# A stack of four graph layers on one core: a list scheduler at build time gives way to a fixed table of places, one round per graph

## The chip, the cores and the metric

The kernel runs on one NeuronCore of a Trainium2 chip. The metric is the device time in microseconds of one execution. Before the change it is 4071.69 us, the median of 3 runs (4068.57 to 4076.79). The five engines are TensorE (PE in the profile; PEld is its loading of weights), VectorE (DVE), ScalarE (ACT), GpSimd (POOL) and SyncE (SP), which here only issues transfers.

## The reference

32 graphs, each with 512 nodes of 256 features and a dense 512 x 512 matrix of edges, pass through four layers. Each layer adds to its input:

```python
h = maximum(layernorm(x), 0); x = x + gat_4_heads(h, adj, W0, a_src, a_dst)     # layer 0
h = maximum(layernorm(x), 0); x = x + gat_1_head(h, adj, W1, a)                 # layer 1
h = maximum(layernorm(x), 0); x = x + edge_scores(h, adj, a_0..a_3)             # layer 2
h = maximum(layernorm(x), 0); x = x + transformer(h, adj, Wqkv, Wo, W1, W2, ..) # layer 3

gat:         e = leaky_relu(s_i + d_j); softmax of e where adj > 0; attention @ (h W); elu
edge_scores: softmax of leaky_relu((h * a_k) @ h.T), k chosen by adj; attention @ h
transformer: 8 heads of 32 with mask, projection, layernorm, a feed-forward of 1024, layernorm
```

Everything is f32. No graph depends on another.

## The kernel before

All weights stay in SBUF. A graph is 481 *jobs*: a job is one instruction of VectorE, ScalarE or GpSimd, one transfer (or four of one kind) issued by SyncE, or a small group of matmuls. The Python function `quick_path` records the jobs of one graph after another through a `Plan`; nothing is issued while they are recorded. The functions `masks`, `layer0` to `layer3` inside `quick_path` record them, always in the same order, so the n-th job of each graph is the same piece of work.

The tiles that the text names:

- `ps_m` (4 jobs): bf16 transposes of the mask, each emptied by VectorE into `mT`; `m3` is the mask of layer 3.
- `ps_t`, `ps_t3`: f32 transposes of the normalized input (`h0`, `h1`, `h2`, `h3`, `n`); `ps_wh`: the products with W in layers 0 and 1.
- `ps_sp`, `rows`: a row of numbers is sent to DRAM and read back to all partitions (`rows0`, `rows1`).
- `ps_o`: attention times values in layers 0 (65 columns wide), 1 (`ps_o1`, 256) and 2 (`ps_o2`, 257); the profile leaves the number out. Before it stand VectorE's `p` (layers 0 and 1) and, in layer 2, the scores `ps_e` with ScalarE's `y`.
- `ps_qk`, `ps_v`, then eight times `ps_s`, `p` (two exponentials on ScalarE, one product with the mask on VectorE), `ps_to` (sums) and `ps_ct` (context): layer 3's attention. The sums go through DRAM twice to be inverted and spread: `to` -> `to_d` -> `part` -> reciprocal -> `in_d` -> `inv`, and VectorE multiplies `cT` by `inv`.
- `ps_wo`: the output projection, which needs `cT`; then `t`, its norm `n`, `ps_t3`, `tT`, the feed-forward `ps_f1` and `ps_f2` (both `ps_f` in the profile), `u`, `y`, and the transfer to the output.

Buffers come in *kinds* with a fixed number of slots, for instance three for `x` and `mT`, six for `p`, one for `h1`. The eight banks of PSUM are two slots `ps_a`, two slots `ps_b` of two banks each, and one each for `ps_ct` and `ps_to`. All matmuls of layers 0, 1 and 2, the mask transposes and `ps_f2` share the two `ps_a` slots; layer 3's share `ps_b`.

The order comes from `Plan.order`. It is a list scheduler that runs while the kernel is built. It keeps a clock for each engine and a queue of jobs whose predecessors are done, gives each job a duration (`takes`, `ends`), and lets a free engine take the ready job with the lowest key that finds its buffers free. The key is

```python
j.key = (self.start + self.done / self.work + self.later[self.at] / 1000, len(self.jobs))
```

that is, the number of the graph, the progress within a layer's stretch of matmul work, and a number from the table `LATER`, found in advance for each of the 481 jobs. Kinds marked `in_turn` give out their slots in the order in which they were recorded. `Plan.carry_out` then issues the jobs in the planned order of their start, ties each engine's instructions together in that order, and makes the first instruction of a new tenant of a slot wait for the first instruction of the one before. On the chip every engine runs its instructions in this fixed order and waits on semaphores for data of the others. At the end a check of ranges (`ok`) decides whether `general_path` must compute everything again; it does not run on these inputs.

Of the kernel before, what the change touches and what calls it, by code (L numbers as in the profile page):

```python
# [20 lines left out]
P = 128  # L21
# [79 lines left out]
class Home:  # L101


    def __init__(self, kind, name, shape, dtype):
        self.kind, self.name, self.shape, self.dtype = kind, name, shape, dtype
        self.tile, self.slot, self.uses, self.left, self.end, self.wants = None, None, [], 0, 0.0, []


class Kind:


    def __init__(self, pool, tag, slots, in_turn=True):
        self.pool, self.tag, self.in_turn = pool, tag, in_turn
        self.shared = tag in ("ps_a", "ps_b")
        self.free, self.last, self.queue, self.head = [0.0] * slots, [None] * slots, [], 0


class Job:
    __slots__ = ("key", "engine", "takes", "ends", "call", "left", "ready", "after", "homes", "start", "port", "moves")


class Plan:
# [4 lines left out]

    HOP = 0.15
    AGAIN = 0.04
    FIRST, LAST = 1.1, 0.25  # L130


# [5 lines left out]
    def __init__(self, tc, later):  # L138
        self.tc, self.nc, self.later = tc, tc.nc, later
        self.jobs = []  # L140
        self.graph()
        self.stage(0.0, 1.0)

    def graph(self):

        self.at = 0

    def stage(self, start, work):

        self.start, self.work, self.done = start, work, 0.0  # L150

    def tile(self, kind, name, shape, dtype=F32):
        home = Home(kind, name, shape, dtype)
        if kind.in_turn:
            kind.queue.append(home)
        size = int(np.prod(shape[1:]))
        return Part(home, np.arange(shape[0]), np.arange(size).reshape(shape[1:]))

    def put(self, engine, takes, ends, outs, ins, call, port=False, moves=None):


        j = Job()
        self.done += takes if engine == "PE" else 0.0
        j.key = (self.start + self.done / self.work + self.later[self.at] / 1000, len(self.jobs))
        self.at += 1
        j.engine, j.takes, j.ends, j.call, j.port, j.moves = engine, takes, ends, call, port, moves
        j.left, j.ready, j.after, j.homes, j.start = 0, 0.0, [], [], None
        before = set()
# [13 lines left out]

        for h in j.homes:
            if h.kind.shared:
                h.wants += [p.home for p in outs if p.home.kind.in_turn and p.home not in h.wants]
        for k in before:
            k.after.append(j)
        j.left = len(before)
        self.jobs.append(j)
        return j  # L190

    def behind(self, job, earlier):
        earlier.after.append(job)
        job.left += 1

    def order(self):

        engines = ("PE", "DVE", "ACT", "POOL", "SP")
        coming, waiting, free = ({e: [] for e in engines} for _ in range(3))
        free = dict.fromkeys(engines, 0.0)  # L200
        port, wire, now, begun = 0.0, 0.0, 0.0, []
        for j in self.jobs:
            if not j.left:
                heapq.heappush(coming[j.engine], (0.0, j.key, j))

        def slots(j):

            take, then = [], None
            need = [h for h in j.homes if h.slot is None]
            need = list(dict.fromkeys(need + [w for h in need for w in h.wants if w.slot is None]))  # L210
            for h in need:
                kind = h.kind
                if kind.in_turn and kind.queue[kind.head + sum(x.kind is kind for x, _ in take)] is not h:
                    return None, None
                open_ = [
                    s for s in range(len(kind.free))
                    if kind.free[s] <= now and not any(x.kind is kind and y == s for x, y in take)
                ]
                if not open_:
                    return None, [x for x in kind.free if now < x < 1e9]  # L220
                take.append((h, min(open_, key=lambda s: kind.free[s])))
            return take, None

        left = len(self.jobs)
        while left:
            moved, nexts = False, []
            for e in engines:
                if free[e] > now:
                    nexts.append(free[e])
                    continue  # L230
                while coming[e] and coming[e][0][0] <= now:
                    _, key, j = heapq.heappop(coming[e])
                    heapq.heappush(waiting[e], (key, j))
                put_back, j = [], None
                while waiting[e]:
                    key, one = heapq.heappop(waiting[e])
                    take, then = slots(one)
                    if take is not None:
                        j = one
                        break  # L240
                    put_back.append((key, one))
                    nexts += then or ()
                for one in put_back:
                    heapq.heappush(waiting[e], one)
                if j is None:
                    if coming[e]:
                        nexts.append(coming[e][0][0])
                    continue
                moved = True
                left -= 1  # L250
                for h, s in take:
                    h.slot = s
                    if h.kind.in_turn:
                        h.kind.head += 1
                    h.kind.free[s] = 1e9
                j.start = max(now, port) if j.port else now
                free[e] = j.start + j.takes
                if j.port:
                    port = free[e]
                begun.append(j)  # L260
                end = j.start + j.ends
                if j.moves is not None:

                    wire = max(wire, j.start + self.FIRST) + j.moves
                    end = wire + self.LAST
                again = free[e] if e == "PE" else end + self.AGAIN
                end += self.HOP
                for k in j.after:
                    k.left -= 1
                    k.ready = max(k.ready, again if k.engine == e else end)  # L270
                    if not k.left:
                        heapq.heappush(coming[k.engine], (k.ready, k.key, k))
                for h in j.homes:
                    h.left -= 1
                    h.end = max(h.end, end)
                    if not h.left:
                        h.kind.free[h.slot] = h.end
            if not moved:
                nexts = [x for x in nexts if x > now]
                assert nexts, "no job can begin"  # L280
                now = min(nexts)
        self.span = max(j.start + j.ends for j in begun)
        return sorted(begun, key=lambda j: j.start)

    def carry_out(self):
# [3 lines left out]
        for j in self.order():  # L289
            firsts = []  # L290
            for h in j.homes:
                if h.tile is not None:
                    continue
                kind = h.kind
                h.tile = kind.pool.tile(
                    h.shape, h.dtype, tag=f"{kind.tag}_{h.slot}", name=h.name, bufs=1
                )
                firsts.append((kind, h.slot))
# [33 lines left out]
    def dma(self, out, in_, moves):  # L332

        pairs = list(zip(out, in_)) if isinstance(out, list) else [(out, in_)]
        outs = [o for o, _ in pairs if isinstance(o, Part)]
        ins = [i for _, i in pairs if isinstance(i, Part)]
        real = lambda x: x.real() if isinstance(x, Part) else x
        call = lambda: [self.nc.sync.dma_start(real(o), real(i)) for o, i in pairs]
        return self.put("SP", 0.1 * len(pairs), 0.1, outs, ins, call, moves=moves)
# [27 lines left out]
def width(args):  # L367
# [5 lines left out]
LATER = [  # L373
    1743, 142, -2198, 582, -1342, -1423, -2322, 251, -1841, -1403, -2073, -1447, -1660, -546, -493, -862, 379,
    -874, -1735, -1387, -1078, -1245, 1879, 1934, 2313, 2511, 1421, 2599, 2919, 2849, 2122, 2830, 2624, 936,
    355, -400, 931, 2188, 1791, 389, 39, 1624, -2868, 2148, 1709, -920, 969, -2126, 2116, 2900, 2358, 686,
    -2280, 2546, 1408, 2128, 1465, -1811, 2793, 2937, 2731, 1331, -1834, -2962, -1606, 463, -492, 413, -2052,
    -1757, -198, 2759, 2862, 2931, 3000, 669, -1389, -2542, -2160, -1285, -764, 3000, 2630, 2553, 1961, 2215,
    -736, 91, 507, 1842, 626, 3000, 3000, 3000, 2743, 1127, -2304, -431, -1315, 528, 237, 2511, 2181, 2465,
# [989 lines left out]
```

## Time and profile before

| | before |
|---|---|
| time, median of 3 | 4071.69 us |
| span of the profiled run | 4075.2 us |
| mean granted clock of TensorE | 0.962 |
| TensorE busy | 3863.9 us, 95% |
| VectorE, ScalarE, GpSimd busy | 61%, 46%, 20% |
| transferred | 144.62 MB, 35 GB/s |
| matmul instructions | 20294 |

How to read it: an f32 matmul counts as two instructions. Busy time of TensorE contains no waits of more than the gaps shown, but it depends on the clock that was granted: the row PEclk of the page gives that clock in 40 slices of the span, in tenths of full speed. A group of instructions is named by line, engine and operation, with output and inputs. Lines 317, 338, 349 and 351 are the helpers through which all jobs of VectorE, ScalarE and GpSimd (317), all transfers (338), all transposes (349) and all products (351) are issued, so the tile's name tells the groups apart. In an order of time, the square bracket behind an instruction gives the idle time before it and what ended it.

### The profile page before, as it was taken

How to read it: one execution, taken by the hardware profiler on the slowest of the kernel's cores; microseconds unless marked ns; L12 is line 12 of the kernel's file. 1: busy time of each engine (PE TensorE's matmuls, PEld its weight loads, DVE VectorE, ACT ScalarE, POOL GpSimd, SP SyncE). 2: the span in 40 equal slices, each digit the busy share in tenths (PEclk: the TensorE clock that was granted, in tenths of full speed). 3: DMA queues.
4: the chain of work that ended last, by engine and by line, in shares of the span. 5: the costliest groups of instructions: out<-in, count | busy, mean ns of one | idle time of the engine just before them, and what ended most of it. 6: DMA issues, size and time to landing. Idle time of an engine off the chain costs nothing. (4 is left out here: it accounts for less than half of the span.)

```text
span 4075.2 us, 52142 instructions
## 1 busy us (share of the span) xinstructions
PE 3863.9 (95%) x20294; PEld 2427.2 (60%) x20294; DVE 2489.1 (61%) x5115; ACT 1881.6 (46%) x3297; POOL 828.8 (20%) x618
## 2 busy tenths in 40 slices
PE   5899999999999999999999999999999999999986
PEld 4655666655666655666655666655666655666543
DVE  4667656567666567656567656567656567656542
ACT  1345454445444445454445444445444445444442
POOL 0122122122122122122112122112122212122121
PEclk7899999999999999999999999999999999999998
DMA  3111101111101101101101101111101101100000
GB/s 111 42 32 43 32 29 40 37 32 43 32 30 40 37 32 43 32 29 40 37 32 43 32 30 40 38 32 43 32 29 40 38 32 43 32 24 24 17 11 13
DMA packets 99278, 144.62 MB, mean 35 GB/s; under 512 B 29008, under 2 KB 65360, under 8 KB 94928
## 3 DMA queue, kind: packets, MB, share of 16 engines
q1 hardware_dynamic: 92672, 136.22, 10.3%
q10 hardware_dynamic: 6352, 4.99, 0.4%
q8 instruction: 162, 2.65, 0.3%
q14 instruction: 92, 0.75, 0.1%
HBM read 122.96 MB, written 18.22 MB: 35 GB/s over the span
## 5 line engine op out<-in xcount | busy, mean ns | idle before, releaser
L351 PEld LDWEIGHTS ps_o<-wh,p 128*128 128x128 f32 x5120 | 696.9, 196 | 256.0 <-issue 189.0
L351 PE MATMUL ps_o<-wh,p 128*128 128x65 f32 (+1 forms) x5120 | 765.1, 302 | 15.7 <-DVE p L317 7.7
L317 DVE TENSOR_TENSOR p<-p,m 128x2048 f32<-128x2048 f32 x256 | 585.4, 2287 | 112.8 <-ACT p L317 112.6
L317 ACT ACTIVATE p<-ps_s 128x1024 f32<-128x1024 f32 x512 | 496.6, 1021 | 334.0 <-PE ps_s L351 333.9
L317 POOL TENSOR_SCALAR rstd<-mv 128x4 f32<-128x4 f32 x192 | 159.2, 829 | 1985.1 <-DVE mv L317 1950.7
L317 DVE SCALAR_TENSOR_TENSOR p<-rows,rt,mT 128x512 f32<-128x512 f32 x512 | 423.2, 868 | 116.3 <-DMA rows<-rows_d 58.1
L351 PE MATMUL ps_f<-ff_t,f 128*128 128x256 f32 x2048 | 489.0, 379 | 0.0
L351 PE MATMUL ps_f<-tT,ff_t 128*128 128x512 f32 x1024 | 465.4, 599 | 2.6 <-ACT tT L317 2.6
L351 PEld LDWEIGHTS ps_f<-ff_t,f 128*128 128x128 f32 x2048 | 377.2, 190 | 92.4 <-issue 39.0
L317 DVE TENSOR_TENSOR u<-ps_f,n 128x512 f32<-128x512 f32 x64 | 44.3, 692 | 524.9 <-PE ps_f L351 524.9
L351 PEld LDWEIGHTS ps_f<-tT,ff_t 128*128 128x128 f32 x1024 | 192.0, 193 | 206.9 <-issue 184.5
L317 ACT ACTIVATE h<-x,shift,rstd 128x256 f32<-128x256 f32 x512 | 265.6, 591 | 83.7 <-DVE x L317 36.5
L351 PE MATMUL ps_s<-qk 32*128 32x512 f32 x2048 | 296.2, 641 | 1.2 <-ACT p L317 1.1
L351 PE MATMUL ps_to<-p,ones 128*32 128x512 f32 x2048 | 272.1, 603 | 8.7 <-DVE p L317 8.7
L317 ACT ACTIVATE f<-ps_f,ff1b_c 128x512 f32<-128x512 f32 x256 | 161.7, 682 | 256.2 <-PE ps_f L351 256.2
L351 PE MATMUL ps_ct<-p,v 128*32 128x512 f32 x2048 | 269.7, 598 | 0.0
L351 PE MATMUL ps_e<-h2T,ha 128*128 128x512 f32 x512 | 262.4, 625 | 0.4 <-DVE o L317 0.4
L351 PE MATMUL ps_qk<-h3T,wqkv_t 128*128 128x512 f32 x512 | 242.9, 599 | 0.0
L351 PE MATMUL ps_o<-h,p 128*128 128x257 f32 x1024 | 238.3, 380 | 1.8 <-DVE x L317 0.9
L317 ACT ACTIVATE y<-ps_e,nshift 128x512 f32<-128x512 f32 x256 | 162.3, 688 | 126.1 <-PE ps_e L351 126.0
L351 PE MATMUL ps_wo<-wo_t,cT 128*128 128x256 f32 x512 | 192.9, 544 | 27.9 <-DVE cT L317 27.9
L317 ACT COPY wh<-ps_wh 128x258 f32<-128x258 f32 x128 | 47.7, 375 | 360.4 <-PE ps_wh L351 360.4
(114 smaller groups left out, 5021.8 us busy)
## 6 DMA issues: line engine op xcount, KB each, us to landing
adj<-in_adj_dram SPq DMA_DIRECT2D x32, 1024.0 KB
rows<-rows_d SPq DMA_DIRECT2D x32, 1024.0 KB
x<-in_x_dram SPq DMA_DIRECT2D x32, 512.0 KB
rows<-rows_d SPq DMA_DIRECT2D x32, 512.0 KB
inv<-in_d SPq DMA_DIRECT2D x256, 64.0 KB
out_dram<-y SPq DMA_DIRECT2D x32, 512.0 KB
ff_t<-in_L_gnn_W_dram ACTq DMA_DIRECT2D x2, 1024.0 KB
to_d<-to SPq DMA_DIRECT2D x64, 8.0 KB
```

What stands on the lines that cost most here:

```text
L317: return [getattr(unit, method)(*map(real, args), **{k: real(v) for k, v in kw.items()})]
L351: made.append(self.nc.tensor.matmul(*map(real, c[:3]), start=c[3], stop=c[4]))
```

## The change

The planner is gone. Each of the 481 jobs has a fixed *place*, the same for all graphs, in a table `PLACES` found in advance. A round is 100000 places long; graph number b is shifted by b rounds. The jobs are sorted by place and issued in that order. The places run from 0 to 503393, so that a graph is spread over five rounds and in a full round the jobs of five graphs interleave in one pattern that repeats. Slots are given in that order too: a new tenant takes, of the slots whose tenant has no use left, the one whose last use lies furthest back. The purpose is an order that is the same in each round and does not depend on a planner's durations.

```diff
-    def __init__(self, tc, later):
-        self.tc, self.nc, self.later = tc, tc.nc, later
+    def __init__(self, tc, table):
+        self.tc, self.nc, self.table = tc, tc.nc, table
         self.jobs = []
...
+    def graph(self, number):
+
+        self.number, self.at = number, 0
...
-        self.done += takes if engine == "PE" else 0.0
-        j.key = (self.start + self.done / self.work + self.later[self.at] / 1000, len(self.jobs))
+        j.place = (self.number * ROUND + self.table[self.at], self.at)
         self.at += 1
...
         for k in before:
+            assert k.place < j.place, "out of order"
             k.after.append(j)
...
-    def order(self):
...
-        for j in self.order():
+        for number, j in enumerate(sorted(self.jobs, key=lambda j: j.place)):
             firsts = []
             for h in j.homes:
-                if h.tile is not None:
-                    continue
-                kind = h.kind
-                h.tile = kind.pool.tile(
-                    h.shape, h.dtype, tag=f"{kind.tag}_{h.slot}", name=h.name, bufs=1
-                )
-                firsts.append((kind, h.slot))
+                if h.tile is None:
+
+                    kind = h.kind
+                    open_ = [s for s, x in enumerate(kind.homes) if x is None or not x.left]
+                    h.slot = min(open_, key=lambda s: kind.homes[s].used if kind.homes[s] else -1)
+                    kind.homes[h.slot] = h
+                    h.tile = kind.pool.tile(h.shape, h.dtype, tag=f"{kind.tag}_{h.slot}", name=h.name, bufs=1)
+                    firsts.append((kind, h.slot))
+                h.left -= 1
+                h.used = number
...
-LATER = [
-    1743, 142, -2198, 582, -1342, -1423, -2322, 251, -1841, -1403, -2073, -1447, -1660, -546, -493, -862, 379,
...
+ROUND = 100000
+PLACES = [
+    101057, 0, 123766, 132584, 138431, 138431, 129046, 129834, 141740, 143105, 134508, 134509, 144040, 210061,
...
     for b in range(B):
-        plan.graph()
-        plan.stage(b, 20.0)
+        plan.graph(b)
...
-        plan.stage(b + 1.3, 27.0)
         x_t = layer1(b, x_t, mT)
         layer2(b, x_t, mT)
-        plan.stage(b + 2.5, 70.0)
         layer3(b, x_t, m3)
```

Three of the durations that jobs carry were changed as well: the transfer of `rows` (1.25 + 0.5 n for 0.75 + 0.5 n), that of `inv` (0.9 for 0.75) and `ps_s` (1.25 for 1.15). Transfers gained the arguments `takes` and `how`, which no call sets.

## The prediction

> **What bounds the kernel now.** I read the page first, then the stretches of the span, then who waits for whom, and last the order of time in one round.
>
> ```profile
> PE 3863.9 (95%) x20294; PEld 2427.2 (60%) x20294; DVE 2489.1 (61%) x5115; ACT 1881.6 (46%) x3297; POOL 828.8 (20%) x618
> ...
> PEclk7899999999999999999999999999999999999998
> ```
>
> TensorE is the bound: 95% busy, the next engine 61%. Yet its granted clock is never a steady ten tenths. The table by stretch (length, then busy time of each engine, the granted clock after POOL) says where the rest lies:
>
> ```profile
> 0.00:200.00 200.00, 139.84 (x632) 111.06 (x633) 109.63 (x273) 54.34 (x122) 16.37 (x29) 0.80 0.24 78
> 200.00:3800.00 3600.00, 3503.88 (x18701) 2193.95 (x18701) 2280.96 (x4654) 1730.23 (x3023) 760.20 (x552) 0.98 0.11 35
> 3800.00:4075.20 275.20, 220.21 (x965) 122.16 (x963) 98.50 (x189) 97.03 (x153) 52.19 (x37) 0.90 0.05 14
> ```
>
> TensorE idles 60 us while the graphs fill the engines, 96 us in the 3600 us of repetition, 55 us while they drain. What it waits for between 300 and 3700 us (total, times, longest):
>
> ```profile
> PE ps_m L349 <- DVE mT L317: 25.9, 56, 0.7
> PE ps_m L349 <- DVE x L317: 21.5, 43, 0.7
> PE ps_wh L351 <- DVE wh L317: 15.8, 28, 0.6
> PE ps_wo L351 <- DVE cT L317: 15.1, 28, 1.1
> PE ps_wh L351 <- ACT h0T L317: 6.4, 28, 0.2
> PE ps_t L349 <- DVE mT L317: 5.7, 24, 0.2
> ```
>
> The sum is 90.4 us in 28 rounds, 3.2 us each, and all of it in one place of the round:
>
> ```profile
> 2086.08 0.40 PE L349 MATMUL ps_m<-ident_b,m 128*128 128x128 bf16 x4 [0.25 <-DVE x L317]
> 2087.13 0.40 PE L349 MATMUL ps_m<-ident_b,m 128*128 128x128 bf16 x4 [0.65 <-DVE x L317]
> 2087.78 0.38 PE L349 MATMUL ps_m<-ident_b,m 128*128 128x128 bf16 x4 [0.26 <-DVE mT L317]
> 2088.83 0.38 PE L349 MATMUL ps_m<-ident_b,m 128*128 128x128 bf16 x4 [0.67 <-DVE mT L317]
> ...
> 2090.97 5.78 PE L351 MATMUL ps_wo<-wo_t,cT 128*128 128x256 f32 x14 [0.43 <-DVE cT L317]
> ```
>
> The four mask transposes run with nothing between them, each waiting for VectorE to empty a bank; then the output projection waits for cT. And it is slow: 14 instructions in 5.78 us are 413 ns each, where 16 of ps_v, the same width, took 3.67 us, 229 ns each. The reason stands in the column after POOL:
>
> ```profile
> 2085.80:2089.20 3.40, 1.57 (x17) 0.97 (x16) 3.40 (x16) 1.79 (x2) 0.00 (x0) 1.00 0.21 64
> 2089.20:2092.60 3.40, 2.74 (x9) 2.08 (x9) 2.49 (x8) 0.00 (x0) 1.27 (x2) 0.50 0.89 274
> 2092.60:2096.00 3.40, 3.40 (x10) 2.68 (x9) 1.24 (x6) 0.00 (x0) 0.00 (x0) 0.50 0.15 55
> ```
>
> One stretch with TensorE 46% busy, and the next 6.8 us run at half clock. In them it is busy 2.74 + 3.40 = 6.1 us, so half of that, 3.1 us, is lost inside "busy" time. The waits cost twice.
>
> **What the Trainium skill says.** "TensorE: Matmul & The Clock Gate", Part 1, section "What's actually happening": the clock is full or half, half after an idle window of about 3.4 us, full again after a busy one. The trace agrees on two states and on the length (6.8 us are two windows), but the window that set it off was 46% busy, not idle. "DMA: Bandwidth & Descriptors", section on the anatomy of one DMA (for the path from gpsimd; here SyncE issues): about 2.0 us fixed, most of it the receipt. Here the copy "to" ended at 2081.52 and the reciprocal of "part", two transfers later, began at 2085.03: at most 1.75 us each. The same section says that the issuing sequencer does the waiting: a transfer that waits holds up those behind it in SyncE's queue.
>
> **The round, in terms.** The wait before ps_wo ends at 256.02 and at 2090.97 us, 15 rounds apart: 122.3 us a round. Less 3.2 idle and 3.1 half clock: 116.0 us of matmul at full clock. For 32 graphs 3712. The middle loses 29 x 6.3 = 183, so filling and draining lose 4075.2 - 3712 - 183 = 180.
>
> **The change, part by part.**
>
> *Removed: the planner at build time.* No instruction of a graph is added or dropped; the counts of matmuls, activations and transfers stay. The numbers handed to the transfers (1.25, 0.9) and to ps_s no longer decide anything, as the order ignores durations. Cost 0.
>
> *Moved: the mask transposes.* In the table the four ps_m stand at places 29046, 34508, 38431 and 41740 of a round, with ps_wo, ps_t, ps_wh and ps_t3 between them. The run of four gaps, 47.4 + 5.7 us over 28 rounds = 1.9 us a round, goes.
>
> *Moved: work into the wait for cT.* From the last ps_to of a graph to ps_wo runs one chain: copy, two transfers, reciprocal, two transfers, multiply. It took from 2080.68 to 2090.91, 10.2 us. Before, there is 5.1 us of matmul after that ps_to (to 2085.8), then the starved transposes. In the new order: two ps_ct (2 x 0.95), four jobs of ps_o2 (4 x 1.73), one ps_m (0.42), the half of ps_wo that needs the other cT (0.44): 9.7 us. So about 0.5 us of wait stays. The chain must not be held up: SyncE's queue has nothing between its four transfers that is late (the first cT's transfers come some 15 us of matmul earlier), and VectorE has x, e and statistics ahead of the reciprocal that end about when "part" lands.
>
> *New waits.* Nobody now takes a later job when one is late; each engine waits at the head of its queue. Behind the multiply that waits for the transfer stand mT, the reciprocals, x and h0T, which free the two ps_a banks. From there to the first ps_f1 VectorE has 53 instructions, 19.1 us by their means, beside 20.3 us of matmul. They follow each other faster than the means say, as they overlap:
>
> ```profile
> 29.77 1.40 DVE L317 BATCH_NORM_STATS2 st<-x 128x6 f32<-128x256 f32 x4
> ```
>
> That is 0.35 us each against a mean of 418 ns. At 0.07 us less each the 53 take 15.4 us. Following the banks in turn, I find gaps of 0.6 (ps_wo), 0.5 (a ps_wh behind t and statistics), 0.3 (ps_t3 behind ScalarE's n), 0.5 (ps_f1 behind tT), and some 0.4 in ps_e and attention: 2.3 us a round. With the full means as spacing it would be 4.6; with only the ps_wo wait, about 0.5. I take 2.3. No 3.4 us then has more than about 1 us idle, against 1.83 before, so I expect no half clock in the middle.
>
> *Fill and drain.* One graph enters per round. The five slices of a graph's matmul are about 0, 17, 15, 32 and 50 us, so full rounds begin after 116 us of matmul, where the old fill had done about 97 by its first ps_s (198 us, counted from the timeline): slice one ends about 68 us, when the timeline of before has the third head's p, as the first graph's chain is unchanged; slice two, with rows1 and p1, about 130; the third, 64 us of matmul with gaps, about 205. That is 89 lost, like before. In the drain attention runs alone in both orders (the old one needed 105 us for the last graph's). I leave 180.
>
> Sum: 3712 + 29 x 2.3 + 180 = 3959; the profiled run was 3.5 us above the median, so **3955 us**, 2.9% less.
>
> **The rivals.**
>
> *A, no loss in the middle is left* (0.3 a round): 3712 + 9 + 180 - 3.5 = 3897. For it: the waits named above vanish from the order. Against: the chain of 10.2 over 9.7, and VectorE's dense stretch.
>
> *B, the forecast, but strict rounds fill and drain worse*, by 60 us: 4015. For it: 89 us lost in fill rests on chains that I only added up; the old order could start a third graph early.
>
> *C, the gaps shrink but the half clock stays.* A stretch from 119.7 us, 88% busy (3.00 of 3.40) with nothing but small ps_o, was enough for it in the fill, and the new order has four ps_o jobs (3.6 us) in a row. 3712 + 29 x (2.3 + 3.1) + 180 - 3.5 = 4045.
>
> *D, slower.* Queues in fixed order jam in the dense stretch: 4.6 us of gaps, the half clock, and 30 us of worse fill: 3712 + 29 x 7.7 + 180 + 30 - 3.5 = 4142. For it: nothing reorders; VectorE is nearly full there. Against: the means overstate it.
>
> **How the numbers follow.** Forecast 0.53 (3925 to 3990), A 0.09, B 0.13, C 0.13, D 0.12. Faster is all but D and a little of C, which reaches to within 0.2% of 4071.7: 0.86, same 0.02, slower 0.12. The range 3900 to 4065 leaves out D and half of A.
>
> **What would show it.** Right: ps_m gone from the waits, the granted clock near 1.0 from 250 to 3750 us, ps_wo's mean down from 544 towards 390 ns, rounds of about 118.3 us, full rounds from about 205 us. Wrong: half clock once a round; a wait of over 2 us at ps_wo; or idle time of over 80 us before 250 or after the last full round.

## The result, and the profile after

| | before | after |
|---|---|---|
| time, median | 4072.15 us (4068.57 to 4076.79) | 3954.2 us (3954.0 to 3955.15) |
| after / before | | 0.971, interval 0.9693 to 0.9727 |
| span of the profiled run | 4075.2 us | 3952.2 us |
| one round, from a graph's first `ps_wo` to the next graph's, mean of 27 full rounds | 122.5 us | 117.8 us |
| rest of the span (span - 29 rounds) | 523 us | 535 us |

The round is 4.6 us shorter, 29 x 4.6 = 134 us; filling and draining cost some 11 us more. The page of after, first the row of busy times, then the granted clock in 40 slices:

```profile
PE 3784.1 (96%) x20294; PEld 2385.8 (60%) x20294; DVE 2592.2 (66%) x5115; ACT 1891.2 (48%) x3297; POOL 780.9 (20%) x618
...
PEclk7799999999999999999999999999999999999998
```

The slices of the clock look as before, since they are cut to whole tenths; the table by stretch (length, busy time of each engine, granted clock) tells the difference:

```profile
0.00:200.00 200.00, 127.53 (x561) 104.45 (x561) 104.13 (x256) 46.48 (x105) 13.54 (x26) 0.74 0.22 73
200.00:3800.00 3600.00, 3542.28 (x19276) 2221.61 (x19275) 2456.59 (x4803) 1799.17 (x3126) 737.91 (x573) 1.00 0.11 36
3800.00:3952.20 152.20, 114.34 (x458) 59.71 (x458) 31.46 (x60) 45.54 (x66) 29.43 (x19) 0.86 0.04 12
```

In the middle TensorE is idle for 58 us instead of 96, and its clock is full (1.00 for 0.98). The record of the clock in the two traces says the same: between 300 and 3700 us, before has 27 stretches at half clock, most of them 6.8 us long, and after has none. In the first 200 us it did 127.5 us of work where it did 139.8 before. What it still waits for between 300 and 3700 us (total, times, longest), 43.7 us in all, 1.6 a round where it was 3.2:

```profile
PE ps_wh L242 <- ACT rt L208: 14.0, 28, 0.5
PE ps_f L242 <- ACT tT L208: 10.7, 28, 0.4
PE ps_t L240 <- ACT h L208: 6.4, 28, 0.2
PE ps_wo L242 <- DVE cT L208: 5.8, 19, 0.5
PE ps_sp L240 <- ACT rt L208: 4.8, 28, 0.2
PE ps_wh L242 <- DVE h1T L208: 1.7, 1, 1.7
```

And the order of time where the starved transposes stood:

```profile
2033.80 5.49 PE L242 MATMUL ps_o<-h,p 128*128 128x257 f32 x24
2039.12 0.39 PE L240 MATMUL ps_m<-ident_b,m 128*128 128x128 bf16 x4
2039.34 0.65 PE L242 MATMUL ps_wo<-wo_t,cT 128*128 128x256 f32 x2
2040.16 0.70 PE L242 MATMUL ps_wo<-wo_t,cT 128*128 128x256 f32 x2 [0.17 <-DVE cT L208]
...
2048.22 1.16 PE L242 MATMUL ps_wh<-w_t,h0T 128*128 128x264 f32 x4 [0.50 <-ACT rt L208]
```

So 1.6 of the 4.6 us a round come from shorter waits; the other 3.0 are about what the half clock cost, which the prediction put at 3.1. In the round shown, the wait for cT is 0.17 us where it was 0.43 behind 1.83 us of other waits. The group of `ps_wo` takes 396 ns an instruction instead of 544, that of `ps_m` idles 9.9 us in all instead of 60.8.

### The profile page after: what moved, and what is told of

Same layout as the page of the kernel before. It is cut to its first block, busy times and chain, and to the rows that moved or that the text cites. A ratio compares the mean times of both kernels' runs of the same rounds, so it can differ in the third digit from the quotient of the medians.

```text
span 3952.2 us, 51981 instructions
## 1 busy us (share of the span) xinstructions
PE 3784.1 (96%) x20294; PEld 2385.8 (60%) x20294; DVE 2592.2 (66%) x5115; ACT 1891.2 (48%) x3297; POOL 780.9 (20%) x618
## 5 line engine op out<-in xcount | busy, mean ns | idle before, releaser
L242 PEld LDWEIGHTS ps_o<-wh,p 128*128 128x128 f32 x5120 | 707.4, 198 | 251.2 <-issue 184.9
L242 PE MATMUL ps_o<-wh,p 128*128 128x65 f32 (+1 forms) x5120 | 762.5, 303 | 27.1 <-DVE p L208 27.1
L208 POOL TENSOR_SCALAR rstd<-mv 128x4 f32<-128x4 f32 x192 | 105.4, 549 | 2490.0 <-DVE mv L208 2197.7
L242 PE MATMUL ps_f<-tT,ff_t 128*128 128x512 f32 x1024 | 455.5, 600 | 13.7 <-ACT tT L208 13.7
L242 PE MATMUL ps_f<-ff_t,f 128*128 128x256 f32 x2048 | 457.6, 380 | 0.0
L208 ACT ACTIVATE h<-x,shift,rstd 128x256 f32<-128x256 f32 x512 | 275.1, 593 | 206.8 <-DVE shift L208 121.7
L242 PE MATMUL ps_e<-h2T,ha 128*128 128x512 f32 x512 | 254.0, 619 | 2.5 <-ACT y L208 1.9
L242 PEld LDWEIGHTS ps_o<-h,p 128*128 128x128 f32 x1024 | 188.9, 189 | 79.5 <-issue 54.5
L208 POOL TENSOR_TENSOR rstd<-rstd,nhalf 128x4 f32<-128x4 f32 x192 | 208.3, 1089 | 13.4
L208 DVE BATCH_NORM_STATS2 st<-x 128x6 f32<-128x256 f32 x512 | 205.6, 414 | 8.1 <-DMA x<-in_x_dram 4.9
```

The source lines that it names most:

```text
L208: return [getattr(unit, method)(*map(real, args), **{k: real(v) for k, v in kw.items()})]
L242: made.append(self.nc.tensor.matmul(*map(real, c[:3]), start=c[3], stop=c[4]))
```

## The experiments

The interval is that of the ratio to the kernel before, which ran again beside each group of experiments; its medians lie between 4071 and 4075 us. Round and rest are those of the profiled run, as above; the rest is good to some 2 us.

| | time (us) | ratio | round | rest |
|---|---|---|---|---|
| e1 old pattern, fixed places | 4113.35 | 1.0081 to 1.0119 | 122.5 | 561 |
| e2 e1, transposes spread | 4178.87 | 1.0239 to 1.0279 | 124.5 | 569 |
| e3 e1, two `ps_o2` ahead of them | 4110.16 | 1.007 to 1.011 | 122.4 | 564 |
| e4 both | 4151.45 | 1.0176 to 1.0213 | 123.4 | 571 |
| e5 before, transposes three times | 4030.38 | 0.987 to 0.9922 | 121.0 | 519 |
| e6 after, transposes three times | 3983.18 | 0.9752 to 0.9803 | 118.9 | 534 |
| e7 e4, layer 1's front moved too | 4233.4 | 1.0376 to 1.0416 | 126.3 | 571 |
| e8 planner with the places as keys | 3955.1 | 0.970 to 0.9738 | 118.2 | 525 |
| e9 after, transposes in a run | 4024.33 | 0.9865 to 0.9903 | 120.1 | 538 |
| e10 after, one multiply later | 4034.23 | 0.9883 to 0.9923 | 120.2 | 549 |
| e11 after, layer 1's front later | 4261.42 | 1.0451 to 1.0488 | 128.0 | 545 |
| e12 e8, strict in the middle | 3939.44 | 0.966 to 0.9693 | 117.1 | 543 |

**e1: is it the fixed places, or the pattern?** The planner's order repeats itself in the middle. Folded into one round it gives a table for the new code, with the old pattern.

```diff
-ROUND = 100000
-PLACES = [101057, 0, 123766, ...
+ROUND = 1000000
+PLACES = [the planned starts of one graph, as parts of a round]
```

> The fixed table, but with the places that the planner's own repeating round has (all 481 jobs in the old order, one graph per round). Theory (two spots of the round decide: the run of mask transposes, and too little matmul beside the chain to cT; the half clock follows from both): as the kernel before, about 4080 us (4050 to 4110), ps_m run with gaps, half clock once a round. Rival 1 (a fixed order with slots taken by last use is what helps, not the pattern): 3950 to 3985. Rival 2 (the run of mask transposes alone is the cause): as the theory here.

The round is that of the kernel before to 0.1 us, with the same waits and the same half clock; the 38 us that e1 takes more (the kernel before took 4074.99 beside it) are all in the rest (561 for 523). So fixed places by themselves gain nothing in the middle and cost 1%, 3 us above the theory's range: the first `ps_wo` comes at 270.6 us instead of 246.7. What the change gains comes from the pattern in its table; e8 shows the other half of this.

**e2, e3, e4: is the run of transposes the cause?** Two traits of the new table were put into e1's (the last six digits are the place within the round).

```diff
 # e2: of the four ps_m and their copies, one stays, three go between jobs of ps_wo; the making of m3 goes behind them
 # e3: two jobs of ps_o2 and their readers on VectorE go ahead of the run
 # e4: both
-    ps_m    10: 1330421,  8: 1336332,  4: 1345390      (most of ps_wo: 355143 to 377030)
+    ps_m    10: 1359500,  8: 1370500,  4: 1378000
-    ps_o2  243: 3419067, 246: 3448385      ps_m  6: 1321456
+    ps_o2  243: 3318000, 246: 3326400      ps_m  6: 1328450
```

> As the run before, but three of the four mask transposes moved between the jobs of ps_wo, so that they no longer form a run (their copies and m3 follow them). Theory: nothing gained, since the transposes had stood in the wait for cT: the gap before ps_wo grows from 0.4 to about 4 us a round and the half clock stays: 4060 to 4120 us. Rival 1: as the old pattern within 15 us. Rival 2: gaps and half clock go, 3950 to 3985 us.

> As the old pattern, but the two jobs of ps_o2 that stood behind ps_wo moved ahead of the run of mask transposes (3.5 us of matmul under the chain to cT); the run stays. Theory: the wait for cT goes, the four gaps of the run (1.8 us) stay, and with them the half clock in most rounds: 4010 to 4070 us. Rival 1: as the old pattern within 15 us. Rival 2: as the old pattern within 15 us.

> Both moves at once in the old pattern. Theory: no run of gaps, no wait over 1 us before ps_wo, no half clock in the middle: 3950 to 3990 us, all of the gain from some 20 of 481 places. Rival 1: as the old pattern within 15 us. Rival 2: as the spread alone.

e2, what TensorE waited for:

```profile
PE ps_wo L242 <- DVE cT L208: 85.3, 27, 3.4
PE ps_wh L242 <- DVE wh L208: 23.9, 27, 0.9
```

Spread alone makes it 65 us slower than e1, past the theory's range: the transposes had covered some of the chain to cT, and 3.2 us a round are now spent in one piece. In e3 the wait for cT is gone, and the half clock is down to 15 stretches of 3.4 us. Yet the time is e1's, for new waits take back what that gains; the two jobs had been covering another chain:

```profile
PE ps_t L240 <- ACT n L208: 32.4, 27, 1.2
PE ps_m L240 <- DVE x L208: 20.2, 27, 0.8
PE ps_f L242 <- ACT tT L208: 18.5, 27, 0.8
```

These are 1.2 us a round for the normalized `n` and 0.7 for `tT`, where e1 shows neither. e4 has hardly any half clock left (1.00 in the middle) and still takes 123.4 us a round: 5.9 us of waits, most of them on cT, n, wh, x, tT and f. Its expectation, a time near the new table's, failed altogether. The run of transposes was a place at which the old order's lack of matmul showed; taking it out alone made things worse.

**e5, e6: what is the half clock worth?** Each mask transpose is issued three times, with the same result. That only adds work.

```diff
-plan.matmuls(0.7, *((ps[:, i], m[:, i, cut(j, P)], ident_b) for i in range(NT)))
+plan.matmuls(0.7, *((ps[:, i], m[:, i, cut(j, P)], ident_b) for _ in range(3) for i in range(NT)))
```

> The kernel before, its order untouched, each mask transpose issued three times (the same result written again): 8 more small matmuls in each of four jobs a round, some 0.5 us each by the spacing of transposes. Theory (the clock halves because a 3.4 us window is less than half busy): more work makes the round shorter; the repeats fall largely into the gaps, the half clock goes: 3990 to 4040 us. Rival (the clock halves for another reason, or bf16 transposes do not count as activity): 1 to 2.2 us a round more, 4100 to 4140 us.

> The kernel after with the same repeats, the price of the repeats where no gap takes them: about 2 us a round by theory and rival, 4005 to 4030 us.

In the new order, where TensorE has hardly a gap there, the added work costs 29 us, 1.1 a round (118.9 for 117.8), less than expected. In the old one it takes 42 us off. The middle of e5:

```profile
200.00:3800.00 3600.00, 3517.51 (x19767) 2221.33 (x19768) 2293.87 (x4709) 1747.91 (x3064) 770.89 (x562) 1.00 0.11 35
```

Its clock is 1.00 where it was 0.98: much of the work lies in the gaps, and of the 27 stretches at half clock four are left, of 3.4 us each. "TensorE: Matmul & The Clock Gate" of the Trainium skill (Part 1, "What's actually happening") speaks of idle windows; here a stretch that was half busy was enough, and filling it with useless work paid. e6 alone would have called the transposes a cost.

**e7: is cover for the second chain what e4 lacks?**

```diff
 # on e4: layer 1's front into the stretch between ps_wo and ps_f1
-    h1 123: 2470173   ps_t 127: 2671763, 132: 2522135   ps_wh 140: 2741122, 146: 2711956, 143: 2686421, 137: 2733826
+    h1 123: 2380000   ps_t 127: 2410800, 132: 2407200   ps_wh 140: 2416000, 146: 2418500, 143: 2425500, 137: 2428000
```

> The kernel of e4 (the old pattern as a fixed table, mask transposes spread, two of the ps_o2 jobs moved) with one more of the new table's traits: layer 1's front, the transposes of h1 and the products with h1T (8 small groups of matmul, about 5.4 us), moves into the stretch between ps_wo and the first ps_f1 of another graph. Theory: what was missing in e4 is matmul to lie over two chains at once, the one from the sums to cT and the one from t over its norm to tT. Then the waits of a round fall from 5.8 to about 2.5 us, no half clock comes back, and the time is about 4055 us (4010 to 4080), 70 to 140 below e4; it stays above the new table's, for the strict rounds of the old pattern lose some 40 us in the fill (e1 against the kernel before). Rival: the queues of VectorE and ScalarE jam in that stretch whatever matmul lies beside it: 4140 or more.

The theory fails by 150 us; the time lies on the rival's side (4140 or more). The wait for `n` is gone from the list, as the theory had it, but cT still takes 34.2 us in 27 rounds and wh 25.0, and h0T (22.4) and h1T (17.6) are new. For cT the trace gives the reason: the transfer of `inv` was issued at 2048.83 us, in the new table's kernel 3.45 us pass from that to the multiply, but here the multiply began at 2054.20, 5.4 us later. It stood in VectorE's queue behind readers of `ps_o2`, a mask copy and statistics. That led to e10.

**e10: one instruction's place in VectorE's queue.** TensorE's order is the new table's; only VectorE's queue is changed (the last five digits are the place within the round).

```diff
 # new table, VectorE around the multiply of cT (job 363, place 429525)
-     7: 129834, 250: 329903, 251: 331583, 256: 331714, 254: 332413, 257: 333807
+     7: 129300, 250: 329310, 251: 329320, 256: 329330, 254: 329340, 257: 329350
```

> The new table with one place changed in effect: on VectorE the multiply of cT with inv, which the second half of ps_wo waits for, stands behind the readers of the last ps_o2 bank, the copy of the first mask and three statistics instead of ahead of them, as it stands in the kernel of e7. TensorE's order stays as it is. Theory (the place of the waiting multiply in VectorE's queue decides the wait at ps_wo, and e3, e4 and e7 lost by it): ps_wo waits 1.3 to 2 us a round where it waits 0.2, most of it not made good later: 3980 to 4005. Rival (TensorE's order alone matters, and VectorE catches up): under 3965.

The order of time on VectorE, in after:

```profile
2039.41 0.69 DVE L208 TENSOR_TENSOR cT<-cT,inv 128x512 f32<-128x512 f32 x1 [0.74 <-DMA inv<-in_d]
2040.02 0.42 DVE L208 COPY mT<-ps_m 128x512 bf16<-128x512 bf16 x1
2040.36 0.16 DVE L208 RECIPROCAL inv<-ps_o 128x1 f32<-128x1 f32 x1
```

and in e10, where the last transfer was issued at 2078.22, so that inv is there at about 2078.22 + 3.45 = 2081.67:

```profile
2081.80 0.42 DVE L208 COPY mT<-ps_m 128x512 bf16<-128x512 bf16 x1 [0.86 <-PE ps_m L240]
2082.14 0.16 DVE L208 RECIPROCAL inv<-ps_o 128x1 f32<-128x1 f32 x1
2082.34 0.48 DVE L208 SCALAR_TENSOR_TENSOR x<-ps_o,inv,x 128x256 f32<-128x256 f32 x1
2082.74 1.07 DVE L208 BATCH_NORM_STATS2 st<-x 128x6 f32<-128x256 f32 x3
2083.72 0.68 DVE L208 TENSOR_TENSOR cT<-cT,inv 128x512 f32<-128x512 f32 x1
```

```profile
2084.45 0.70 PE L242 MATMUL ps_wo<-wo_t,cT 128*128 128x256 f32 x2 [2.21 <-DVE cT L208]
```

The multiply is 2.05 us late, and `ps_wo` waits 2.2 us for it where it waited 0.2. Most rounds take 119.8 us, 2.0 more than in after: all of the lateness reaches the end, and nothing is made good later. Every fifth round has 3.4 us of half clock behind the wait besides and takes 121.5, so that the mean is 2.3 more. The whole is +80 us, twice what was expected; 67 of it is 29 x 2.3, the rest is in the fill and the drain.

**e9: the transposes put back in a run, in the new table.**

```diff
-     6: 129046, 10: 134508, 4: 138431, 8: 141740
+     6: 129046, 10: 129070, 4: 129090, 8: 129100      (each with its copy behind it)
-     250: 329903, 251: 331583      (VectorE's readers of the last ps_o2 bank)
+     250: 329060, 251: 329061
```

The copies and the two readers then stand ahead of the multiply of cT in VectorE's queue, so this run holds a part of e10's change too.

> The new table with one thing undone: the four mask transposes stand in a run ahead of ps_wo again, each with VectorE's copy of its bank behind it and the copies ahead of the multiply that makes cT, as in the kernel before. All other places stay. Theory (the run starves TensorE on VectorE's copies and sets off the half clock): some 1.7 us more idle a round at ps_m and ps_wo, a stretch of 3.4 us about half busy, and half clock after it, 3 us more: 3954 + 29 x (1.7 to 4.7) = 4003 to 4090, about 4070. Rival (what the new table gains lies in the rest of its order, and the run costs little in it): under 3985.

```profile
2079.33 0.38 PE L240 MATMUL ps_m<-ident_b,m 128*128 128x128 bf16 x4 [0.52 <-DVE mT L208]
2079.92 0.71 PE L240 MATMUL ps_m<-ident_b,m 128*128 128x128 bf16 x8 [0.21 <-DVE x L208]
2080.47 0.65 PE L242 MATMUL ps_wo<-wo_t,cT 128*128 128x256 f32 x2
2081.82 0.70 PE L242 MATMUL ps_wo<-wo_t,cT 128*128 128x256 f32 x2 [0.69 <-DVE cT L208]
```

The gaps come back, 0.52 and 0.21 at `ps_m` and 0.69 at `ps_wo`, and the time is 70 us longer, on the theory's side. The half clock comes only in every fourth or fifth round, which then takes 121.5 us instead of 119.8. What TensorE waited for at these places, between 300 and 3700 us:

```profile
PE ps_wo L242 <- DVE cT L208: 19.6, 28, 0.9
PE ps_m L240 <- DVE mT L208: 14.4, 28, 0.5
PE ps_sp L240 <- ACT rt L208: 12.8, 28, 0.5
```

With 5.9 us of `ps_m` behind x, 20 us are gaps in the run itself. The 14 us more at `ps_wo` need not be the run's: in the round shown `inv` was issued at 2075.27, so that it was there at about 2078.72, and the multiply began at 2081.10, behind the copies, 2.4 us late as in e10. So in the old pattern spreading the run costs 65 us, and in the new one a run costs something, at most 70; how much of that is the run and how much the late multiply, this run doesn't separate.

**e11: layer 1's front out of the stretch, in the new table.**

```diff
-    123 to 148: 233629 to 240610 (between ps_wo and ps_f1), the row after them 245207
+    123 to 148: 244500 to 249735 (between the ps_f1), the row after them 250200
```

> The new table with layer 1's front (the four activations h1, the transposes of h1, the products with h1T, the row after them) moved from between ps_wo and the first ps_f1 to between the ps_f1, so that 5.4 us of matmul no longer lie beside the chain t, n, ps_t3, tT. Theory (the new order is fast because the chains are covered by other graphs' matmul): ps_t3 and ps_f1 wait some 4 us more a round, and the half clock may come back: 3954 + 29 x (3.5 to 7) = 4055 to 4157, about 4100. Rival (the chain gets shorter by as much, as VectorE and ScalarE lose the work of h1 there): under 4000.

```profile
PE ps_t L240 <- ACT n L208: 50.4, 26, 1.9
PE ps_wh L242 <- DVE h1T L208: 22.7, 26, 0.9
PE ps_wh L242 <- ACT rt L208: 20.4, 26, 0.8
PE ps_f L242 <- ACT f L208: 18.5, 11, 1.7
PE ps_o L242 <- DVE p L208: 18.0, 27, 0.7
```

The wait for `n`, absent in after, is 1.9 us in each round, and the clock falls to 0.97 in the 3600 us of the middle, by which some 100 of the 307 us are half clock (an estimate: 0.03 x 3600). But the theory's 4 us at `ps_t3` and `ps_f1` are 2.2, and the time is 160 us above its middle: most of the waits are where the front now stands (h1T, p, f). The run shows that the front can't be moved by a tenth of a round; it doesn't separate the missing cover from the crowd at the new place.

**e8, e12: a faster version.** e8 is the old list scheduler with the new places as keys; slots are given out in the order of the places too.

```diff
-j.key = (self.start + self.done / self.work + self.later[self.at] / 1000, len(self.jobs))
+j.key = (self.number * ROUND + PLACES[self.at], self.at)
```

> The old list scheduler with the new table's places as its keys: a free engine may take a later job when the one in turn isn't ready, so the first and last rounds are filled greedily, while the repeating part keeps the new table's order but for some 6 inversions a round on TensorE, 31 on ScalarE and 150 on VectorE. Theory: strict rounds cost the fill some 20 to 40 us, and the order by place is what makes the middle fast: 3920 to 3950. Rival: the planner's durations are off in the middle, so the exchanges on VectorE bring waits back, 1 to 3 us a round: 3960 to 4020, with the fill shorter all the same.

Its rest is that of the old kernel (525), and it loses 0.3 us a round, so that nothing is left: 3955.1, between the theory and its rival. Together with e1 this settles where the gain lies: the old scheduler reaches the new time with the new places, and the new code keeps the old round with the old ones. e12 keeps each engine strictly in order of place from place 360000 to 3350000, and moves layer 3's weights, with the few instructions that prepare them, from ScalarE's queue to SyncE's.

```diff
+if FROM <= j.key[0] < TO:
+    if j.engine in last: self.behind(j, last[j.engine])
+    last[j.engine] = j
...
-    nc.scalar.dma_start(t, ap)       # wqkv, wo, ff1, ff2 and layer 3's vectors
+    nc.sync.dma_start(t, ap)         # issued behind the first graph's input
```

> An attempt at a faster version. The places as in the new table, strict on every engine from the fourth round to the last graph's, but the first and last rounds filled by the old list scheduler with the places as keys (as in e8, where the repeating part lost 0.3 us a round by being reordered as well); and the weights of layer 3 are fetched by SyncE behind the first graph's input instead of by ScalarE, whose first activation of a graph waited until 25.1 us for the issue of all of them. Expected: 7 us from the first graphs, 3 from the last, 5 from the weights: 3936 to 3948. Rival (a gain in the fill is swallowed by the next graph's wait, as in e8): 3950 to 3957.

The time came in as expected, 3939.4, the fastest of all, and for another reason: the rest is 543 us, 8 more than after, and the round is 117.1 us, 0.8 less. The weights gained nothing. The first graph's `ps_sp` runs at 30.5 instead of 36.5 us, but the row it sends goes through SyncE's queue with small weight transfers on both sides:

```profile
32.26 0.35 SPq L366 DMA_DIRECT2D rows_d<-spr  x1
32.65 0.42 SPq L40 DMA_DIRECT2D b_c<-in_L_gnn_ln_b_dram  x1
...
34.10 0.43 SPq L40 DMA_DIRECT2D g_r<-in_L_gnn_ln_g_dram  x1
34.63 0.38 SPq L366 DMA_DIRECT2D rows<-rows_d  x1
```

VectorE's first `p`, which needs it, began at 42.06 us, against 43.21 in after: 1.1 of 6 us are left. From the issue of `rows` to `p` it took 7.4 us (34.63 to 42.06), in after 4.7 (38.47 to 43.21), and from the issue of `rows_d` to that of `rows` 2.4 us instead of 1.4. Whether the queue or the DMA engines themselves held the row up, the run doesn't show: from 32 to 43 us the engines were 71% busy.

The shorter round comes from one stretch. From the second half of `ps_wo` to the first `ps_f1` TensorE takes 16.3 us in after (2040.16 to 2056.42) and 15.5 in e12 (2149.32 to 2164.80), which is the whole 0.8. What differs there is when ScalarE waits. In after:

```profile
2047.31 0.18 ACT L208 ACTIVATE wh<-ps_wh 128x4 f32<-128x4 f32 x1 [0.31 <-PE ps_wh L242]
2047.98 0.18 ACT L208 ACTIVATE rt<-ps_wh 128x8 f32<-128x8 f32 x1 [0.49 <-DVE wh L208]
```

and in e12:

```profile
2156.03 0.18 ACT L345 ACTIVATE wh<-ps_wh 128x4 f32<-128x4 f32 x1 [0.31 <-PE ps_wh L379]
2156.10 0.18 ACT L345 ACTIVATE rt<-ps_wh 128x8 f32<-128x8 f32 x1
```

Both engines read one bank of `ps_wh`, and they take turns in the order in which the program issues them. The table has VectorE's product `wh` (place 135221) ahead of ScalarE's `rt` (135696), so ScalarE, which waits in order, stands still for 0.49 us four times a round, and `ps_wh`, `ps_t` and `ps_sp` wait behind it (0.50, 0.23 and 0.17 us in after). e12 issues by planned start, `rt` first; each engine's own order is unchanged, and these waits of TensorE are gone but for 0.36 us behind VectorE. "PSUM — Partial Sum Buffer" ("PSUM bank collisions raise a hardware error") says that the compiler puts a dependency between two engines' accesses to one bank, reads by ScalarE and VectorE alike; the 0.49 us fit that. The exchange of the two places alone was not run, so that it makes the whole 0.8 us is not shown; e12 also gives out its slots differently.

## Why the prediction was right

3955 was forecast and 3954.2 measured. That it is right to 1 us is luck, for three small errors cancel. The gaps were smaller than forecast, 29 x (1.8 - 2.3) = -15 us for the profiled span (1.8 is the round of 117.8 less 116.0 of matmul). Fill and drain were larger, 3952.2 - 3712 - 29 x 1.8 = 188 for 180. And the 3.5 us taken off at the end were a trait of the one profiled run of before, the slowest; in after the span is 2.0 us below the median, 5.5 us the other way. What holds is the mechanism: the run of gaps and the half clock go, and small waits take their place.

- *116.0 us of matmul a round*: holds; 117.8 less the 1.6 us of waits is 116.2.
- *The run of transposes goes, and the half clock with it*: holds in after, where `ps_m` is out of the list and the middle runs at 1.00. As a cause by itself it is too simple. e2 shows that taking out the run alone makes the old pattern slower; e9 shows that with the rest of the new table in place it is worth something: 20 us of gaps are its own, and 70 us is the most.
- *A chain of 10.2 us over 9.7 us of matmul, 0.6 of wait at ps_wo*: it waited in 19 of 28 rounds, 0.2 us on average. The condition that the prediction put beside it, that the multiply must not be held up, carried the result: e10 breaks it and loses 80 us, and e9 breaks it too.
- *The other gaps*: `ps_f1` behind tT 0.4 for 0.5. `ps_wh` 0.5 for 0.5, but not because VectorE's queue is dense with statistics: it is the turn-taking at the bank, which the prediction didn't know. `ps_t3` behind `n` none for 0.3, attention none for 0.4; `ps_t` behind h (0.2) and `ps_sp` behind rt (0.2) were not foreseen. That the sum came close owes something to luck.
- *Nobody takes a later job when one is late*: right, and seen in e10, where 2 us of lateness cost 2.0 us in most rounds and half clock besides in every fifth.
- *The fill*: full rounds were forecast from about 205 us, at a loss of 89; by the places they began at about 235, at a loss of 119 with the same 116 us of matmul (the slices that the prediction names add up to 113). In the fill TensorE waits 27.1 us for `p` behind the transfer of rows, up to 7.4 at a time, which the sum of slices left out. The drain gave much of it back: the last two distances between `ps_wo` are 104 and 92 us, before 108 and 101. Rival B was right in its direction, with 8 us for 60.
- *Rivals*: A's empty middle was not reached, though e12 came 0.8 us a round nearer. C's half clock didn't stay. D's jams didn't come with this table, but e7 and e11, each a few dozen places away from one table or the other, have them.

## What to carry to other kernels

In a steady pattern of several graphs, ask of each wait what lies over it and what that work covered before it was moved: here spreading one run of transposes made one table slower, and undoing the spread made the other slower. Look up, in the queue of the engine that produces the last operand, what stands ahead of that one instruction; one multiply behind six others cost 2%. Where two engines read one bank, look which read the program issues first; e12 suggests, but does not show, that exchanging the two pays.

## What was not expected of the hardware

- How busy TensorE is in a stretch of 3.4 us doesn't alone decide whether half clock follows. One with 1.98 us of work was followed by it in e9, which is more than the half that e5's theory named; in e10 one with 1.70 us of work was not, and one with 1.28 was (length, busy time of each engine, granted clock; first e9, then e10):

```profile
755.20:758.60 3.40, 1.98 (x20) 1.27 (x18) 2.83 (x10) 0.00 (x0) 0.58 (x1) 1.00 0.02 5
758.60:762.00 3.40, 3.40 (x10) 2.63 (x11) 0.83 (x3) 0.60 (x1) 1.04 (x1) 0.51 0.00 0
...
881.20:884.60 3.40, 1.70 (x9) 1.45 (x10) 2.13 (x8) 0.60 (x1) 0.00 (x0) 1.00 0.02 5
884.60:888.00 3.40, 3.40 (x23) 3.00 (x22) 2.21 (x9) 1.75 (x4) 0.00 (x0) 1.00 0.00 0
...
1000.60:1004.00 3.40, 1.28 (x7) 1.13 (x8) 2.55 (x8) 0.60 (x1) 0.04 (x1) 1.00 0.00 0
1004.00:1007.40 3.40, 3.40 (x13) 2.79 (x12) 1.41 (x6) 1.25 (x3) 0.00 (x0) 0.50 0.02 5
```

- The same gap, repeated in every round, brought half clock only in every fifth round of e10. In the traces every stretch of one clock in the middle is a multiple of 3.41 us long, and a round of 119.8 us is 35.1 of these steps, so the gap falls differently into them from round to round. That it has to fill enough of one step fits this; it was not tested.
- The half clock can cost more than the work that keeps it off: tripling the transposes took 42 us off the old order, and added 29 to the new one, which had no half clock in the middle to lose.
- Two readers of one bank on different engines took turns, at 0.49 us for a read of 128x256 by VectorE ahead of one of 128x8 by ScalarE.
